# A two-step graph layer with guessed top-p thresholds: one store per pair of key and query tiles, sums stored a slot later, law constants by step with a round less, and the last products of a guess on VectorE

## The chip, the cores and the metric

The kernel runs on one core of one Trainium2 chip. The metric is the device time of one execution in microseconds (us). A core has five engines that each work through their own queue in order: PE (TensorE, matrix products; PEld is its weight load), DVE (VectorE), ACT (ScalarE), POOL (GpSimd) and SP (SyncE, which here only issues DMAs). They wait for each other through semaphores.

## The reference, cut to what matters

```
h = relu(layernorm(x))                       # x: 3327 x 256, adj: 3327 x 3327, sparse
R = (adj + I) / rowsum                       # fixed graph
for n in range(2):
    q = Xa @ W1.T @ W2.T ; k = Xa @ W3.T     # 64 columns each
    probs = softmax(q @ k.T)                 # 3327 x 3327
    A = the largest probs of each row until their sum reaches 0.9, renormalised
    Xf = R @ Xf ; Xa = A @ Xa
    Z += Xf @ U1[n].T + Xa @ U2[n].T
out = x + layernorm(h + Z)
```

For each row of the attention matrix the threshold has to be found from which on values are kept.

## The kernel before, in words

The 3327 rows are padded to 3328 and cut into 26 tiles of 128 rows (`NT` = 26). Two steps run one after the other, and each passes through the 26 tiles in slots of some 21 to 24 us, as a software pipeline in which several tiles are under way at once: exps of a later tile's logits (`weights`, L634 products on PE and L636 exp on ACT), the guess of the next tile (`measured_once` in step 0, `measured_twice` in step 1), the settling of the present one (`settle`), and the attention sum of the one before (`Sums`, L836 transposes and L849 products on PE). `settle` is where the exact threshold is found on DVE: one pass over the row block keeps in `w` what lies below the guess (L756), 20 MAX8 take the eight largest of each segment (L761), then rounds of MAX8 and MATCH_REPLACE (L768, L770) draw the largest 8 candidates at a time, 5 rounds in step 0 and 6 in step 1 (`ROUNDS`); a scan and three small operations (L775 to L780) find the boundary, and a second pass over the block masks it (L790). The guess itself is a law of the row's logarithm sum with constants `PG`, `PK`, `OFFSET`, `LNY`. In step 1 it has two stages: the last ones are ACT's third pass over the block (L660), two small operations on DVE (L726, L727), two on POOL (L724, L725: column 0 of `g`), three Ln-type operations on ACT (L729 to L731), two on DVE (L733, L734), five products on POOL (L735 to L739) and the exp on ACT (L741) that L756 waits for.

If a row's boundary isn't among the drawn candidates, a flag (`prove`) sends the whole program through `search_graph_layer`, a bisection of 27 rounds per tile.

In the opening a loop over `q` normalises x, and makes keys and queries of tile pairs: products on PE, `kq` copied on DVE, high parts cast on ACT, low parts subtracted on DVE. Each pair's raw queries go to `asks` (turned to the other half of the partitions) and its split queries to `qx` by DMAs on ACT's queue; `fetch` brings `qT` of a tile back. Meanwhile SP loads pieces of the adjacency (832 KB each at first), and DVE lists each row's nonzero blocks (`listed`, L879). After the opening the `products` (L1039 on PE) fill the free time of the first slots.

POOL also gathers (L926, L947: indirect DMAs that it issues itself), normalises the output (`finish`, L994 to L997 and L481 to L987), and adds `sv` (L972), which SP stores at once (L974).

In the slots the order on every engine is written by hand: `PLAN`, `BEGIN`, `OPEN` and `LAST` name for each of a slot's seven parts which generators (letters: m guess, d settle, f finish, g gather, s spread, e first_end, ...) go on by one `yield`, and every engine's instructions are tied to that order. In the opening a list scheduler places them.

Of the kernel before, what the change touches and what calls it, by code (L numbers as in the profile page):

```python
# [9 lines left out]
F32 = mybir.dt.float32  # L10
F32R = mybir.dt.float32r
# [3 lines left out]
AF = mybir.ActivationFunctionType  # L15
ALU = mybir.AluOpType
# [3 lines left out]
P = 128  # L20
N = 3327
# [293 lines left out]
LNBIG = 69.0  # L315
SEG = 168
NSEG = -(-NP // SEG)
ROUNDS = (5, 6)
PG = (0.72168716, 3.51308980, -3.48705157)
PK = (3.57528079, -2.54929187, 0.86603878)  # L320
OFFSET = (18.0, 14.0)
TOPK = 8 * max(ROUNDS)
LNY = 0.25 * math.log(0.72)

SQG, SQK = ((c[0], c[1] / (2 * c[0]), c[2] - c[1] ** 2 / (4 * c[0])) for c in (PG, PK))
HALF = NT // 2
# [10 lines left out]
AD = 4  # L337
# [10 lines left out]
def guess_graph_layer(ctx, tc, x, adj, w1t, w2t, w3t, u1t, u2t, ln_g, ln_b, out, flag):  # L348
    nc = tc.nc
# [74 lines left out]
    law = const.tile([P, 7, NT], F32, tag="law", name="law")  # L424
    one = const.tile([P, 8], F32, tag="one", name="one")
    for k, c in enumerate((1.0, -1.0, 5.0e-4, SQG[1], SQK[1], math.log(10.0), LNY, 1.0e-12)):
        G.memset(one[:, k : k + 1], c)
    of_s = const.tile([P, 4], F32, tag="of_s", name="of_s")
    for k, c in enumerate((SQG[0], SQG[2], -SQK[0], -SQK[2])):
        G.memset(of_s[:, k : k + 1], c)  # L430
    ones = const.tile([P, 1], F32, tag="ones", name="ones")
# [26 lines left out]
    kx = dram.tile([P, NP], F32, tag="kx", name="kx")  # L458
    qx = dram.tile([P, NP], F32, tag="qx", name="qx")
    qm = const.tile([P, 2, 2, 2 * DA + 2], F32, tag="qm", name="qm")  # L460
    G.memset(qm, 0.0)
# [96 lines left out]
    def project(step, t):  # L558
# [14 lines left out]
        G.tensor_tensor(col(2), col(1), half[:, 1:2], ALU.pow)  # L573
        G.tensor_scalar(ms[:, 3:7], of_s, col(2), 1.0e-4, ALU.mult, ALU.add)
        G.tensor_scalar(col(7), col(1), 0.5, minus, ALU.mult, ALU.subtract)
        G.tensor_scalar(col(7), col(7), 0.25, LNY - 0.25 * math.log(0.1 / N), ALU.mult, ALU.add)
        G.tensor_scalar(col(8), col(1), minus, col(4), ALU.subtract, ALU.add)
# [3 lines left out]
    def laws(ts):  # L581
# [19 lines left out]
        S.activation(s, s, AF.Exp, scale=0.5)  # L601
        for k, c in ((3, SQG[0]), (4, SQG[2]), (5, -SQK[0]), (6, -SQK[2])):
# [3 lines left out]
        G.tensor_scalar(m, m, 0.25, LNY - 0.25 * math.log(0.1 / N), ALU.mult, ALU.add)  # L606
        G.tensor_scalar(var, var, 0.125, None, ALU.mult)
# [34 lines left out]

    def guessed(r, g):
# [6 lines left out]
        S.activation(col(2), col(2), AF.Exp, scale=-1.0, bias=con(6))  # L650
        S.activation(col(3), col(2), AF.Square, bias=con(3))
# [10 lines left out]
    def measured_once(r):  # L662
        e, ms = r["e"], r["ms"]


        col = guessed(r, small.tile([P, 17], F32, tag="g", name="g"))
        S.activation(col(4), col(2), AF.Square, bias=con(4))
# [27 lines left out]
    def measured_twice(r):  # L695
# [3 lines left out]

        col = guessed(r, small.tile([P, 18], F32, tag="g", name="g"))  # L700
        S.activation(col(1), col(0), AF.Exp, scale=-1.0, bias=con(5))
# [32 lines left out]
        V.reciprocal(col(12), col(12))  # L734
# [4 lines left out]
        G.tensor_tensor(col(6), col(6), col(15), ALU.add)  # L739
        yield  # L740
# [222 lines left out]
    def first_end(t):  # L963
# [9 lines left out]
        yield  # L973
        nc.sync.dma_start(sx[t], sv)  # L974
        yield from prep(aT, t)
# [83 lines left out]
    scaled, turned, made, raw = {}, {}, {}, {}  # L1059
    for q in range(HALF + 5):  # L1060
        if 0 <= q - 3 < HALF:
            k, pk = q - 3, made.pop(q - 3)
            kq = row.tile([P, 2, P], F32, tag="s1", name="kq", bufs=4)
            qs = row.tile([P, 2, P], F32R, tag=("own", "xa")[k % 2], name="qs", bufs=2)
            V.tensor_copy(kq, pk[:, :2, :])
            raw[k] = kq, qs
            if 2 * k in COUNTED:
                V.tensor_copy(krs[:, k % 2, :DA], pk[:, 2, :DA])
# [33 lines left out]
        if 0 <= q - 3 < HALF:  # L1102
            kq, qs = raw[q - 3]
            S.copy(keys[low, 2 * (q - 3) * P : (2 * (q - 3) + 2) * P], kq[low].rearrange("p t r -> p (t r)"))
            S.copy(qs[high], kq[high])
        if 0 <= q - 4 < HALF:
            k, (kq, qs) = q - 4, raw[q - 4]
# [3 lines left out]
        if 0 <= q - 5 < HALF:  # L1111
            k, (kq, qs) = q - 5, raw.pop(q - 5)
# [16 lines left out]
        if q == 5:  # L1129
            for n in range(2):  # L1130
                nc.sync.dma_start(u1[:, :, n], u1t[n].rearrange("(c p) e -> p c e", p=P))
    moments(0, pgram[:DA, : DA + 1])
    for k in range(3):
# [201 lines left out]
```

## Time and profile before

| what | value |
| --- | --- |
| time, median of 3 runs | 1377.66 us (1375.54 to 1378.56) |
| the profiled execution, its own time | 1375.91 us |
| its span in the trace | 1374.2 us |
| busy: PE, DVE, ACT, POOL | 1237.3, 1197.8, 1074.3, 1026.1 us |
| mean granted TensorE clock | 0.972 |

The stages by the trace: opening until the first `w` (L756) at 93.1 us, the first slots with the products until 208 us, step 0 until about 762 us, step 1 from there, with its last `w` at 1326.6 us. In the page, part 1 gives the busy time of each engine, part 4 the chain of work that ended last, part 5 groups of instructions with mean durations in ns. A row of the chain or of the timeline begins with its start in us and its length in us.

### The profile page before, as it was taken

What the parts mean: (1) busy time and instruction counts of PE and PEld (TensorE: products, weight loads), DVE (VectorE), ACT (ScalarE), POOL (GpSimd) and SP (SyncE); (2) the same over time, 40 slices, a digit from 0 to 9 for tenths busy, and PEclk for the clock granted to TensorE, in tenths of its full rate; (3) what the DMA queues carried; (4) which work ended last, traced back from release to release, by engine and by line L of the source; (5) the groups of instructions that cost most, each with busy time, mean ns of one, the idle gap of its engine ahead of it and who ended that gap; (6) DMA issues with size and microseconds to landing.
All of it is one profiled execution on the core that took longest, in us unless ns stands there. A gap on an engine that the chain in (4) does not pass through costs nothing.

```text
span 1374.2 us, 22501 instructions
## 1 busy us (share of the span) xinstructions
PE 1237.3 (90%) x6340; PEld 1030.9 (75%) x6340; DVE 1197.8 (87%) x3662; ACT 1074.3 (78%) x2239; POOL 1026.1 (75%) x1437
## 2 busy tenths in 40 slices
PE   5769899999999999999999669898999999999985
PEld 4534688888887888888788558787878778787874
DVE  7757789999999999999892589898998999999993
ACT  4566688878787887878763689898998999998841
POOL 4123588888888888888785578888887888888842
PEclk9789999999999999999999869999999999999998
DMA  8644455555555555555544321322313133131200
GB/s 287 216 128 128 144 166 142 155 159 152 169 152 163 148 163 149 154 163 157 149 144 121 87 58 57 94 85 66 97 54 96 61 94 92 59 97 55 85 24 23
DMA packets 123192, 164.60 MB, mean 120 GB/s; under 512 B 21137, under 2 KB 89232, under 8 KB 123056
## 3 DMA queue, kind: packets, MB, share of 16 engines
q1 hardware_dynamic: 100608, 117.19, 27.4%
q0 software_dynamic: 16640, 42.69, 11.9%
q10 hardware_dynamic: 5808, 3.17, 0.8%
q8 instruction: 53, 0.87, 0.2%
q14 instruction: 83, 0.68, 0.2%
HBM read 128.74 MB, written 32.12 MB: 117 GB/s over the span
## 4 chain that ended last, share of the span: by engine, by line
DVE 53%; PE 17%; ACT 16%; POOL 7%; issue 4%; DMA 2%; SPq 0%; ACTq 0%; DVEq 0%; POOLq 0%
DVE cand L761 9%; ACT ja L660 9%; DVE w L756 8%; DVE e L790 8%; PE pa L849 6%; DVE fm L879 5%; DVE bb L768 4%; DVE cand L770 4%; PE pz L1039 2%; PE pl L634 2%; ACT e L636 2%; PE pt L836 2%; PE pr L955 2%; POOL g L739 1%; ACT eT L838 1%
## 5 line engine op out<-in xcount | busy, mean ns | idle before, releaser
L660 ACT ACTIVATE ja<-e,g 128x3328 uint8<-128x3328 f32 x106 | 325.9, 3075 | 0.1
L849 PE MATMUL pa<-x,eT 128*128 128x256 f32 x1352 | 321.9, 379 | 0.0
L849 PE MATMUL pa<-xw,eT 128*128 128x256 f32 x1352 | 318.3, 380 | 3.1 <-DVE s L979 3.1
L849 PEld LDWEIGHTS pa<-xw,eT 128*128 128x128 f32 x1352 | 251.5, 190 | 36.4 <-DVE s L979 5.0
L849 PEld LDWEIGHTS pa<-x,eT 128*128 128x128 f32 x1352 | 242.8, 190 | 25.5
L761 DVE MAX8 cand<-w 128x8 f32<-128x168 f32 (+1 forms) x1040 | 253.4, 317 | 0.0
L838 ACT COPY eT<-pt 128x512 f32<-128x512 f32 (+1 forms) x364 | 199.3, 555 | 58.7 <-PE pt L836 58.5
L947 POOL DMA_INDIRECT xg<-bx,index x130 | 192.8, 1483 | 51.5 <-issue 21.1
L836 PE MATMUL pt<-ident,e 128*128 128x128 f32 x1144 | 175.3, 276 | 46.3 <-DVE e L790 32.4
L634 PE MATMUL pl<-keys,qT 128*128 128x512 f32 (+1 forms) x832 | 198.9, 375 | 17.3 <-ACT e L636 12.2
L836 PEld LDWEIGHTS pt<-ident,e 128*128 128x128 f32 x1144 | 140.4, 144 | 87.1 <-issue 50.0
L926 POOL DMA_INDIRECT ac<-in_adj,index x130 | 159.8, 1229 | 57.5 <-ACT e L1045 16.3
L947 POOL DMA_INDIRECT xg<-vx,index x130 | 150.6, 1159 | 34.2 <-issue 33.2
L634 PEld LDWEIGHTS pl<-keys,qT 128*128 128x128 f32 x832 | 144.2, 194 | 42.0 <-ACT e L636 14.4
L636 ACT ACTIVATE e<-pl 128x832 f32<-128x832 f32 (+1 forms) x176 | 150.5, 862 | 31.4 <-PE pl L634 27.3
L756 DVE SCALAR_TENSOR_TENSOR w<-e,g 128x3328 f32<-128x3328 f32 x44 | 163.8, 3722 | 4.7 <-ACT g L741 4.6
L955 PE MATMUL pr<-xg,ac 128*128 128x257 f32 (+1 forms) x520 | 140.2, 394 | 10.0 <-DVE s L1162 8.4
L790 DVE SCALAR_TENSOR_TENSOR e<-e,rec 128x3328 f32<-128x3328 f32 x40 | 148.0, 3701 | 0.6
L955 PEld LDWEIGHTS pr<-xg,ac 128*128 128x128 f32 x520 | 96.3, 197 | 22.1 <-DVE s L1162 8.8
L768 DVE MAX8 bb<-cand 128x8 f32<-128x160 f32 x286 | 92.6, 324 | 6.4
L879 DVE TENSOR_REDUCE fm<-at 128x4 f32<-128x512 f32 (+1 forms) x133 | 84.3, 634 | 5.9 <-DMA at<-in_adj 5.9
L703 POOL TENSOR_SCALAR g<-g,law 128x1 f32<-128x1 f32 x23 | 65.8, 2862 | 10.9 <-ACT g L702 10.0
(261 smaller groups left out, 2018.6 us busy)
## 6 DMA issues: line engine op xcount, KB each, us to landing
at<-in_adj SPq DMA_DIRECT2D x114, 256.0 KB
cx<-ac SPq DMA_DIRECT2D x26, 384.0 KB
ac<-cx SPq DMA_DIRECT2D x26, 384.0 KB
wide<-in_adj SPq DMA_DIRECT2D x8, 832.0 KB
qT<-qx SPq DMA_DIRECT2D x196, 32.0 KB
e<-in_adj SPq DMA_DIRECT2D x6, 832.0 KB
own<-bx SPq DMA_DIRECT2D x26, 128.5 KB
x<-in_x SPq DMA_DIRECT2D x13, 256.0 KB
```

The lines of the kernel that those rows point to most:

```text
L634: PE.matmul(pl[:, a:b], qT[:, k, :], keys[:, c + a : c + b], start=k == 0, stop=k == 1)
L636: S.activation(e[:, c : c + w], pl[:, :w], AF.Exp, accum_out=za[:, n : n + 1])
L660: S.activation(ja, e, f, bias=guess, scale=sign, accum_out=total)
L756: V.scalar_tensor_tensor(w, e, col(16), e, ALU.is_lt, ALU.mult, accum_out=d2)
L761: V.max(cand[:, 8 * s : 8 * s + 8], w[:, s * SEG : min(NP, (s + 1) * SEG)])
L790: V.scalar_tensor_tensor(e, e, at(1), e, ALU.is_ge, ALU.mult, accum_out=ra)
L836: PE.transpose(pt[:, j, :], e[:, (j0 + j) * P : (j0 + j + 1) * P], ident)
L838: S.copy(eT[:, :w, :], pt[:, :w, :])
L849: PE.matmul(self.pa, eT[:, c - 4 * k, :], self.xa[:, c, :], start=c == 0, stop=c == NT - 1)
L926: G.indirect_dma_start(out=ac[:, k, :], out_offset=None, in_=rows, in_offset=bass.IndirectOffsetOnAxis(ap=index[:, t, k : k + 1], axis=0), ...
L947: G.indirect_dma_start(out=xg[:, k, :w], out_offset=None, in_=rows, in_offset=bass.IndirectOffsetOnAxis(ap=index[:, t, k : k + 1], axis=0))
L955: PE.matmul(pr[:, :w], ac[:, k, :], own if k == KT - 1 else xg[:, k, :w], start=k == 0, stop=k == KT - 1)
```

## The change

Five edits:

- A pair's raw and split queries now lie in one tile `both` of 2 KB a partition, and go to `rx` in one store per pair on SP, a pass of the loop later. `asks` is read back from `rx` (`recall`), `qT` of step 0 as well. `fetch` takes two DMAs instead of four. ACT issues no DMAs in the loop any more.
- The store of `sv` joins the list that SP works off in a later part of the slot (`stores`).
- `PG`, `PK`, `OFFSET`, `LNY` are given per step, and `ROUNDS` goes from (5, 6) to (4, 5).
- The five last products of the guess in step 1 move from POOL to DVE, with narrower bounds, and in another order.
- The first logits of tile 0 come one pass of the loop later.

```
-ROUNDS = (5, 6)
-OFFSET = (18.0, 14.0)
+ROUNDS = (4, 5)
+OFFSET = (16.0, 13.0)
...
-    def fetch(step, t, q2=None, by=nc.sync):
+    def fetch(step, t):
         qT = tpool.tile([P, 2, P], F32R, tag="qT", name="qT", bufs=3)
+        of = qx[:, t * P : (t + 1) * P] if step else rx[:, t // 2, 2 + t % 2, :]
         for rows in (low, high):
-            for k, half_ in enumerate((low, high)):
-                src = qx[half_, t * P : (t + 1) * P] if q2 is None else q2[half_].bitcast(F32)
-                by.dma_start(qT[rows, k, :].bitcast(F32), src)
+            nc.sync.dma_start(qT[rows].bitcast(F32), of.rearrange("(k p) r -> p k r", k=2))
+    def recall(a, b):
+        for h, rows in enumerate((high, low)):
+            nc.sync.dma_start(asks[rows, a:b, :], rx[high, a:b, h, :])
...
         V.reciprocal(col(12), col(12))
-        G.tensor_scalar(col(12), col(12), col(8), 0.7, ALU.mult, ALU.max)
-        G.tensor_scalar(col(11), col(12), 1.5, col(11), ALU.min, ALU.mult)
-        G.tensor_tensor(col(2), col(3), col(2), ALU.subtract)
-        G.tensor_scalar(col(15), d1, col(0), LNBIG, ALU.is_lt, ALU.mult)
-        G.tensor_tensor(col(6), col(6), col(15), ALU.add)
+        V.tensor_scalar(col(12), col(12), col(8), 0.85, ALU.mult, ALU.max)
+        V.tensor_scalar(col(11), col(12), 1.2, col(11), ALU.min, ALU.mult)
+        V.tensor_scalar(col(15), d1, col(0), LNBIG, ALU.is_lt, ALU.mult)
+        V.tensor_tensor(col(6), col(6), col(15), ALU.add)
+        V.tensor_tensor(col(2), col(3), col(2), ALU.subtract)
...
-        nc.sync.dma_start(sx[t], sv)
+        stores.append((sx[t], sv))
...
-    for q in range(HALF + 5):
+    for q in range(HALF + 6):
...
-            kq = row.tile([P, 2, P], F32, tag="s1", name="kq", bufs=4)
-            qs = row.tile([P, 2, P], F32R, tag=("own", "xa")[k % 2], name="qs", bufs=2)
+            both = (tpool.tile([P, 4, P], F32, tag="eT", name="both", bufs=3) if k % 5 < 3 else
+                    adjp.tile([P, AD, P], F32, tag="at", name="both", bufs=2))
...
-            for h in range(2):
-                nc.scalar.dma_start(query_of(2 * k + h), kq[high, h, :])
-            nc.scalar.dma_start(qx[:, 2 * k * P : (2 * k + 2) * P], qs.bitcast(F32).rearrange("p t r -> p (t r)"))
-            for h in range(2):
-                if 2 * k + h < 3:
-                    fetch(0, 2 * k + h, qs[:, h, :], nc.scalar)
+        if 0 <= q - 6 < HALF:
+            nc.sync.dma_start(rx[:, q - 6], raw.pop(q - 6)[0])
+        if q in (7, 8):
+            for t in range(2 * (q - 7), 4 * q - 26):
+                fetch(0, t)
+        if q == 15:
+            recall(0, 7)
...
-        if q == 6:
+        if q == 7:
             run(begun[0], 1)
```

Lines move by 5 or 6 in the changed file, so before's L724, L725, L734, L790 are its L729, L730, L739, L795. On SP, in the opening, this stood before (x is the input, wide and e hold pieces of the adjacency, u is a weight):

```order
L389 DMA x_95<-in_x 128x2x256 x13
L869 DMA wide<-in_adj 128x1664 x2
L1131 DMA u_138<-in_u1t 128x2x256 x2
L869 DMA e_101<-in_adj 128x1664 x2
L869 DMA wide<-in_adj 128x1664 x2
L869 DMA e_101<-in_adj 128x1664 x2
```

and this stands there now, with a store of a pair behind each piece of the adjacency:

```order
L874 DMA e_101<-in_adj 128x1664
L1118 DMA rx<-both 128x512
L874 DMA e_101<-in_adj 128x1664
L1118 DMA rx<-both 128x512
L551 DMA qT<-rx 64x2x128 x4
L874 DMA wide<-in_adj 128x1664
L1118 DMA rx<-both 128x512
L551 DMA qT<-rx 64x2x128 x2
```

So loads, stores and fetches now share one queue in the opening. On DVE, in a slot of step 1, this stood behind the reciprocal of the guess before (bb and cand are the candidates of `settle`; in brackets, whom the instruction waits for):

```order
L734 RECIPROCAL g<-g 128x1 [waits DVE_49]
L768 MAX bb<-cand 128x8
L770 MATCH_REPLACE cand<-bb,cand 128x160 [waits DVE_49]
L768 MAX bb<-cand 128x8 [waits DVE_49]
L770 MATCH_REPLACE cand<-bb,cand 128x160 [waits DVE_49]
L768 MAX bb<-cand 128x8 [waits DVE_49]
```

and this stands there now:

```order
L739 RECIPROCAL g<-g 128x1 [waits DVE_49]
L740 TENSOR_SCALAR g<-g 128x1 [waits DVE_49,Pool_49]
L741 TENSOR_SCALAR g<-g 128x1 [waits DVE_49,Pool_49]
L742 TENSOR_SCALAR g<-g 128x1 [waits Pool_49]
L743 TENSOR_TENSOR g<-g 128x1 [waits DVE_49]
L744 TENSOR_TENSOR g<-g 128x1 [waits Activation_49]
L773 MAX bb<-cand 128x8
L775 MATCH_REPLACE cand<-bb,cand 128x160 [waits DVE_49]
L773 MAX bb<-cand 128x8 [waits DVE_49]
```

One round has gone from behind them, and the products stand in DVE's queue ahead of the rest of `settle`. What they wait for on POOL is, in its own queue now, the end of this piece (rstd and nm belong to the output's normalisation, xg to the gathers):

```order
L952 DMA xg<-vx,index 128x256 [waits DMASW6_49]
L721 TENSOR_SCALAR g<-g 128x1 [waits Activation_49]
L722 TENSOR_SCALAR g<-g 128x1
L723 TENSOR_SCALAR g<-rec,g 128x1 [waits DVE_49]
L724 TENSOR_SCALAR g<-g 128x1
L483 TENSOR_SCALAR rstd<-mv 128x1 [waits DVE_49]
L484 TENSOR_TENSOR rstd<-rstd,half 128x1 [waits Pool_49]
L992 TENSOR_SCALAR nm<-mv,rstd 128x1 [waits Pool_49]
L729 TENSOR_SCALAR g<-oa 128x1 [waits Activation_49]
L730 TENSOR_SCALAR g<-rec,g 128x1 [waits Pool_49]
```

The piece is as it was; only the five products that followed it have gone from POOL.

More of the change, by code (lines that the diff above doesn't have):

```diff
@@ L424, in guess_graph_layer @@
     law = const.tile([P, 7, NT], F32, tag="law", name="law")
-    one = const.tile([P, 8], F32, tag="one", name="one")
-    for k, c in enumerate((1.0, -1.0, 5.0e-4, SQG[1], SQK[1], math.log(10.0), LNY, 1.0e-12)):
+    one = const.tile([P, 10], F32, tag="one", name="one")
+    for k, c in enumerate((1.0, -1.0, 5.0e-4, SQG[0][1], SQK[0][1], math.log(10.0), LNY[0], 1.0e-12, SQG[1][1], LNY[1])):
         G.memset(one[:, k : k + 1], c)
-    of_s = const.tile([P, 4], F32, tag="of_s", name="of_s")
-    for k, c in enumerate((SQG[0], SQG[2], -SQK[0], -SQK[2])):
-        G.memset(of_s[:, k : k + 1], c)
+    of_s = const.tile([P, 2, 4], F32, tag="of_s", name="of_s")
+    for step in range(2):
+        for k, c in enumerate((SQG[step][0], SQG[step][2], -SQK[step][0], -SQK[step][2])):
+            G.memset(of_s[:, step, k : k + 1], c)
     ones = const.tile([P, 1], F32, tag="ones", name="ones")
@@ L638, in weights, with guessed @@
                 yield
-    def guessed(r, g):
+    def guessed(r, g, step):
         r["col"] = col = lambda k: g[:, k : k + 1]
@@ L663, in measured_once @@
         e, ms = r["e"], r["ms"]
-        col = guessed(r, small.tile([P, 17], F32, tag="g", name="g"))
+        col = guessed(r, small.tile([P, 17], F32, tag="g", name="g"), 0)
         S.activation(col(4), col(2), AF.Square, bias=con(4))
@@ L696, in measured_twice @@
         e, ms = r["e"], r["ms"]
-        col = guessed(r, small.tile([P, 18], F32, tag="g", name="g"))
+        col = guessed(r, small.tile([P, 18], F32, tag="g", name="g"), 1)
         S.activation(col(1), col(0), AF.Exp, scale=-1.0, bias=con(5))
@@ L1131, in guess_graph_layer @@
                 nc.sync.dma_start(u1[:, :, n], u1t[n].rearrange("(c p) e -> p c e", p=P))
+    recall(7, HALF)
     moments(0, pgram[:DA, : DA + 1])
```

30 lines of the change are left out of this document (15 added, 15 removed).

## The prediction

> **What bounds the kernel now.** I read the page's chain of work first, to see which engine ended last, and then the busy time by stage, cut at the `w` passes (L756) that open the slots.
>
> ```profile
> span 1374.2 us, 22501 instructions
> DVE 53%; PE 17%; ACT 16%; POOL 7%; issue 4%; DMA 2%; SPq 0%; ACTq 0%; DVEq 0%; POOLq 0%
> ```
>
> ```profile
> 0.00:93.10 93.10, 58.17 (x238) 41.08 (x238) 66.18 (x196) 48.57 (x102) 28.87 (x120) 0.88 0.72 229
> 93.10:208.30 115.20, 107.95 (x458) 76.37 (x459) 88.31 (x262) 82.28 (x189) 62.14 (x78) 0.96 0.45 135
> 208.30:663.40 455.10, 443.69 (x2382) 376.69 (x2380) 439.21 (x1372) 376.92 (x891) 385.22 (x461) 1.00 0.55 156
> 663.40:808.00 144.60, 115.46 (x585) 95.95 (x585) 97.92 (x343) 93.19 (x201) 98.68 (x142) 0.90 0.39 113
> 808.00:1326.60 518.60, 479.25 (x2519) 413.07 (x2518) 480.30 (x1416) 465.70 (x845) 441.56 (x621) 0.99 0.25 76
> ```
>
> A row has the stretch, its length, the busy time of PE, PEld, DVE, ACT and POOL, the granted clock, the DMA share and GB/s. No engine bounds the opening alone. From 93 to 208 us PE is full (107.95 of 115.20). In step 0 the chain runs on DVE, but PE is idle only 455.10 - 443.69 = 11.41 us in 19 slots: two engines are near their bound. Step 1 runs from 808.0 to 1326.6 us in 24 slots, 518.60 / 24 = 21.61 us each (24 by the count of a group shown below), with DVE busy for 480.30 of it.
>
> The sum below is made against the profiled execution, 1375.9 us (its span and 1.7 us around it). The median of the runs is 1.8 us higher, and I add that at the end.
>
> **Step 0: a round less.** A round stands in the chain of step 0 like this:
>
> ```profile
> 208.39 3.62 DVE w L756 x2
> ...
> 224.60 0.40 DVE cand L770 x2
> 225.00 0.02 issue
> 225.02 0.34 DVE bb L768
> 225.36 0.02 issue
> ...
> 232.35 3.62 DVE w L756 x2
> ```
>
> The change takes 0.40 + 0.02 + 0.34 + 0.02 = 0.78 us from each slot of 23.96 (232.35 - 208.39). If DVE alone decided, 19 slots would give 14.8 us. PE's transposes show what is late next:
>
> ```profile
> L836 PE MATMUL pt<-ident,e 128*128 128x128 f32 x494 | 76.8, 275 | 11.4 <-DVE e L790 7.2 <-ACT kq L515 4.3
> ```
>
> Nearly all of PE's idle time in these slots, 11.4 us, lies before this group, and 7.2 us of it ends with DVE's mask. A faster DVE can shrink that part; the 4.3 us that end with ACT stay, unless ACT's work comes earlier with DVE's. So the gain is between 4 us, should PE's waits shrink by half, and 11.4 us; I take 6, a little under the 7.2.
>
> **Step 0: the sums stored later.** One slot at the end of step 0 is longer:
>
> ```profile
> 639.40:663.40 24.00, 24.00 (x132) 20.41 (x130) 23.14 (x74) 19.64 (x45) 18.09 (x22) 1.00 0.52 147
> 663.40:690.50 27.10, 22.55 (x120) 18.82 (x120) 22.87 (x66) 20.02 (x49) 23.38 (x28) 1.00 0.51 146
> ```
>
> ```profile
> 664.08 4.19 POOL sv L972
> 668.29 0.32 SPq L974
> ...
> 671.15 3.63 DMA at<-in_adj
> 674.80 0.69 DVE fm L879
> ```
>
> SP stands behind the sum `sv`, which POOL finishes late, and the piece of the adjacency behind it reaches DVE late. With the store moved to the later part of the slot, SP issues that load without waiting for `sv`; queued behind the store afterwards are the key and query stores of the same list, which nothing in the slot waits for. What can go is the slot's excess of 27.10 - 24.00 = 3.1 us; PE was idle 27.10 - 22.55 = 4.55 there, so PE lets it go. I take 3, with 0 as the other end. In the other slots the load isn't late and the move costs and gives nothing: SP waits hide behind buffers already loaded. So step 0 gives 9.
>
> **The opening.** The chain of the opening waits for DMAs five times:
>
> ```profile
> 22.57 4.49 DMA asks<-kq
> 28.39 6.84 DMA qT<-qs
> 35.26 2.04 DMA qT<-qs
> 46.54 4.08 DMA asks<-kq
> 55.01 2.40 DMA asks<-kq
> ```
>
> ```profile
> 0.00:34.00 34.00, 20.11 (x85) 14.49 (x86) 24.04 (x77) 13.76 (x28) 15.92 (x78) 1.00 0.87 286
> 34.00:69.00 35.00, 25.45 (x112) 19.77 (x113) 28.12 (x80) 20.39 (x43) 6.43 (x20) 0.76 0.69 216
> ```
>
> They are 19.85 us, the most that could go. Of these the 8.88 of `qT` are the plainest: the fetches were issued on ACT, so ACT stood still with its copies, and now SP does it. The other three are waits for a buffer whose store hasn't landed; the new tile has such a wait too. The queues themselves set the other bound. By the two rows 34 x 286 + 35 x 216 KB, 17.3 MB, moved in the first 69 us. The change adds 64 KB to each of 13 pairs and reads 0.85 MB back for `asks`, but one piece of the adjacency (0.85 MB) comes after the loop now instead of in it: 18.1 MB, which at 286 GB/s take 63 us. So of the 69 us about 6 can go. SP then holds the rest of `recall` behind a fetch that waits for tile 0's products, so the later side is 0, or a loss of 4 (one late DMA such as the 4.08). I take a gain of 6, and keep -4 to 15.
>
> The rule that speaks against this edit is in the Trainium skill, "DMA: Bandwidth & Descriptors", section "Queues, rings and completion order": a DMA engine takes turns between queues packet by packet, but works through one queue's ring in order. By that rule a store on ACT's queue took turns with the loads, and on SP's it lies behind the pieces of the adjacency issued ahead of it, so the opening would gain nothing; that is the second rival below, which I price from rows.
>
> **Step 1: the products on DVE.** This is the term that turns the sign. The chain of one slot, and POOL and ACT beside it:
>
> ```profile
> 958.85 3.60 DVE w L756 x2
> 972.73 0.16 DVE g L734
> 975.84 3.70 DVE e L790 x2
> 979.73 3.60 DVE w L756 x2
> ```
>
> ```profile
> 958.92 3.60 POOL L704 TENSOR_SCALAR g<-g 128x1 f32<-128x1 f32 x1
> ...
> 973.99 0.27 POOL L725 TENSOR_SCALAR g<-rec,g 128x1 f32<-128x1 f32 x1
> ...
> 995.23 0.27 POOL L725 TENSOR_SCALAR g<-rec,g 128x1 f32<-128x1 f32 x1
> ...
> 996.86 3.55 POOL L739 TENSOR_TENSOR g<-g 128x1 f32<-128x1 f32 x1
> ```
>
> ```profile
> L725 POOL TENSOR_SCALAR g<-rec,g 128x1 f32<-128x1 f32 x24 | 6.5, 270 | 2.4
> L727 DVE TENSOR_SCALAR g<-g 128x1 f32<-128x1 f32 x24 | 5.1, 214 | 0.8
> 976.77 0.28 ACT L702 ACTIVATE g<-g,one 128x1 f32<-128x1 f32 x1
> ```
>
> What the move removes: in the next slot L739, an operation on one column, runs while DVE does L790, and takes 3.55 us; `w` then starts late. Without such a delay a slot is 979.73 - 958.85 = 20.88 us, so at most 0.73 of the mean 21.61 hangs on it.
>
> What it adds: a wait. Of the five products now on DVE, the third (before's L738, the flag of `d1`) reads the column that POOL's L725 writes. In the shown slot the reciprocal L734 ends at 972.89, and L725 ends at 974.26. DVE fills 0.43 us with the first two products (two small operations of 0.214), then stands until 974.26, some 0.9 us; queued behind are the last two rounds, the scan, the mask L790, and the next `w`. Until now POOL bore this wait, and DVE did three rounds meanwhile.
>
> The new slot, counted from its `w` at 958.85: L725 ends at 974.26; three more products 0.64 bring 974.90. From the reciprocal to L790 there were 975.84 - 972.89 = 2.95 us; a round less makes 2.17, so the mask starts at 977.07. From mask to `w` it is 3.89 as before: 980.96. The slot is 22.11 us, 0.50 over the mean, and 24 slots lose 12.0 us. ACT isn't late: the exp L741 comes behind L702, which ended at 977.05, and `w` needs it at 980.96. The slot's shape also holds for the next slot: L703 on POOL starts after L702, at 977.05, so it is caught by the mask again, L704 by `w`, and POOL's row of operations up to L725 starts after `w`'s end as it did in the shown one.
>
> The bounds: if POOL came early enough that DVE never waits, the slot is 20.88 - 0.78 + 5 x 0.214 = 21.17, a gain of 10.6. If every slot is like the next one (`w` at 979.73, L725 ending at 995.50), it is 995.50 + 0.64 + 2.17 + 3.89 - 979.73 = 22.47, a loss of 20.6. I take the middle one, since the row of POOL's operations between `w` and L725 is not touched by the change.
>
> At the two ends of the steps one more slot each, outside the counted ones, loses its 0.78 us of a round; with the narrower scan behind it I take 2 us. The law's constants change no instruction count. Worked through with the reference's inputs in double precision, at most 30 values are drawn until the boundary in step 0 (of 32) and 35 in step 1 (of 40), so the second program isn't entered. If it were, each of its rounds has a pass like this one:
>
> ```profile
> L660 ACT ACTIVATE ja<-e,g 128x3328 uint8<-128x3328 f32 x106 | 325.9, 3075 | 0.1
> ```
>
> and 27 rounds x 26 tiles x 2 steps x 3.075 us alone are 4317 us.
>
> **The sum.** -6 (opening) - 9 (step 0) - 2 (ends) + 12 (step 1) = -5 us: 1370.9 for the profiled execution, some 1372.5 as a median; I give 1372.
>
> **The rivals.**
>
> 1. *DVE is held longer in step 1* (slower). The mechanism is the same wait, at the price of the later slots: 22.47 us each, 20.6 in place of 12, so 1381; with an opening that gives nothing, 1387. It decides from 22.3 us a slot (a loss of 17 eats the other terms). For it: L725 comes 1.37 us behind the reciprocal in one slot and 1.73 in the next. Against: the later one follows from a late L703, which itself follows from products on POOL that go.
> 2. *The opening gains nothing* because the stores lie behind the loads in one queue: a piece of 832 KB takes 2.9 us at 286 GB/s, and a pair's tile, one of five, is written again when its store has landed. The price is the opening's 6 us, so 1378, no change. For it: the DMA share of 0.87 in the first 34 us. Against: the share of 0.69 behind that.
> 3. *DVE doesn't wait in step 1*, since POOL has five operations less per slot and gets ahead: -10.6 in place of +12, 1350. For it: POOL is idle 518.60 - 441.56 = 77 us in 24 slots, so it isn't full. Against: its operations from `w`'s end to L725 follow each other and DVE's two long passes stop it.
> 4. *The second program is entered*, since the law misses a row: 1372 + 4317, over 5,600 us. Against it are the counts above; nothing in the profile is for it.
>
> **How the numbers follow.** My forecast has 0.42, the first rival 0.25, the second 0.20, the third 0.12, the fourth 0.01. A measurement of this kernel can tell about 0.2%, 2.8 us, from no change. Of the forecast's own range (1364 to 1380) 0.30 lie below 1374.9, 0.08 within, 0.04 above; of the second rival 0.06, 0.08 and 0.06; of the first 0.02 within and 0.23 above; the third is faster. That gives faster 0.48, same 0.18, slower 0.34. The range takes in the first rival to 1386 and the opening's better end (9 us more), with part of the third: 1357 to 1386.
>
> **What the profile after would show.** Step 0: slots of 23.5 to 23.7 us, and PE's idle time before L836 down from 11.4 us by half or more. The slot at 663 us as long as its neighbours. Opening: the first `w` at some 87 us, with no wait of ACT for `qT`. Step 1: idle time of DVE before the product that reads POOL's column, 0.8 to 1.0 us in each of 24 slots, released by that POOL operation, slots of 22.1 us, and no POOL operation of 3.55 us in the guess's products. Wrong it would be made by that idle time being near 0 (then rival 3), or by slots of 22.4 us and more (rival 1).

## The result, and the profile after

The changed kernel takes 1385.18 us (median of 5 runs, 1383.64 to 1387.28), the kernel before 1376.80 us beside it (1375.54 to 1378.56). The ratio is 1.006, with a 95% interval of 1.0045 to 1.0075: the change makes the kernel slower by 8.4 us. The forecast was 1372 us. The profiled execution of the changed kernel took 1385.18 us, so nothing has to be added to its trace.

The first lines of the page of the changed kernel, with the chain's shares by engine:

```profile
span 1383.5 us, 22295 instructions
DVE 43%; PE 26%; ACT 11%; POOL 4%; issue 3%; DMA 1%; SPq 0%; DVEq 0%; ACTq 0%; POOLq 0%
```

DVE's share fell from 53% to 43%, PE's rose from 17% to 26%: the path moved, but did not become shorter. The stages of the changed kernel, cut at the same `w` passes as before (the columns are those of the prediction):

```profile
0.00:98.70 98.70, 65.24 (x256) 43.69 (x257) 66.66 (x196) 55.00 (x120) 30.24 (x130) 0.84 0.70 233
98.70:204.30 105.60, 98.35 (x432) 70.49 (x431) 86.83 (x252) 74.68 (x165) 59.70 (x73) 0.98 0.52 152
204.30:655.80 451.50, 442.99 (x2367) 375.79 (x2366) 429.66 (x1315) 375.79 (x892) 382.56 (x458) 0.99 0.56 157
655.80:804.10 148.30, 122.21 (x610) 101.57 (x609) 96.47 (x341) 94.49 (x207) 102.65 (x141) 0.89 0.38 108
804.10:1336.70 532.60, 490.86 (x2516) 426.44 (x2515) 479.76 (x1465) 470.11 (x844) 413.73 (x495) 0.96 0.25 74
```

Read against before's rows: the fifth `w` comes at 204.3 instead of 208.3; the 19 slots of step 0 take 451.5 instead of 455.1; what lies between them and step 1's slots 148.3 instead of 144.6; the 24 slots of step 1 532.6 instead of 518.6. By the terms of the prediction, in us (step 0 counted over its 21 slots up to the last `w`, 503.55 before and 500.89 after; the ends are the passage between the steps and what follows the last `w`):

| term | forecast | measured |
| --- | --- | --- |
| opening, up to the fifth `w` | -6 | -4.0 |
| step 0 (a round 6, the late slot 3) | -9 | -2.7 |
| ends of the steps | -2 | +2.0 |
| step 1, 24 slots | +12 | +13.9 |
| sum | -5 | +9.3 |

**Step 1** has the wait that was worked out, in about half of its slots. Three rows of DVE's timeline in a slot whose `w` starts at 1116.54, and the group of the waiting product:

```profile
1131.07 0.21 DVE L741 TENSOR_SCALAR g<-g 128x1 f32<-128x1 f32 x1
1132.04 0.21 DVE L742 TENSOR_SCALAR g<-g 128x1 f32<-128x1 f32 x1 [0.76 <-POOL g L730]
...
1134.63 3.69 DVE L795 SCALAR_TENSOR_TENSOR e<-e,rec 128x3328 f32<-128x3328 f32 x1
```

```profile
L742 DVE TENSOR_SCALAR g<-g 128x1 f32<-128x1 f32 x24 | 5.0, 209 | 11.7 <-POOL g L730 11.7
```

DVE stands 0.76 us in that slot in front of the third product until POOL's column arrives, and everything behind it, the mask L795 and the next `w`, is late by that. It does so in 13 of the 24 slots, 11.7 us in all; most of these 13 last 21.9 us. In ten slots, one of the 13 among them, DVE waits for PE before it takes over PE's sums `pa` (a line of waits has the us in total, the times and the longest):

```profile
DVE s L984 <- PE pa L854: 12.5, 10, 2.0
```

Each of these ten begins with a low granted clock, behind a pause of 2.0 us or more in which PE waits for the late mask. This is PE in the slot that follows the one above, and the first 4 us of that slot:

```profile
1138.47 1.48 PE L841 MATMUL pt<-ident,e 128*128 128x128 f32 x8 [2.02 <-DVE e L795]
```

```profile
1138.50:1140.50 2.00, 2.00 (x10) 1.90 (x11) 2.00 (x2) 1.10 (x2) 1.93 (x2) 0.62 0.00 0
1140.50:1142.50 2.00, 2.00 (x8) 1.71 (x8) 1.94 (x4) 1.03 (x3) 1.92 (x2) 0.53 0.00 0
```

It lasts 22.3 us. The mean of all 24 is 22.19 us; 22.11 were forecast, from the first wait alone.

**The opening**: SP's longest wait for another engine, and DVE's two waits for the adjacency, until the first `w`:

```profile
SPq L551 <- PE pl L639: 13.0, 1, 13.0
```

```profile
DVE fm L884 <- DMA e<-in_adj: 8.2, 1, 8.2
...
DVE fm L884 <- DMA wide<-in_adj: 4.7, 1, 4.7
```

The change also fetches the queries of tiles 3 to 5 in the opening, which their slots fetch anyway. The fetch for tile 3 needs tile 0's buffer, so SP stands 13.0 us until PE has done tile 0's products, and the pieces of the adjacency behind it come late. The 8.2 us are new; a wait for a piece in `wide` stood in the kernel before too (4.2 us). The first `w` starts at 98.7, not at 87.

**Step 0** has three long slots, at 463, 629 and 656 us (25.5, 27.1 and 26.4 us), where before had one. POOL's addition of the identity in the slot ahead of the second of them and in it, then DVE's mask and ACT's waiting operation in it, by the timeline:

```profile
621.36 0.49 POOL L937 TENSOR_TENSOR ac<-ac,ident 128x128 f32<-128x128 f32 x1
...
645.89 3.69 POOL L937 TENSOR_TENSOR ac<-ac,ident 128x128 f32<-128x128 f32 x1
```

```profile
645.58 3.68 DVE L795 SCALAR_TENSOR_TENSOR e<-e,rec 128x3328 f32<-128x3328 f32 x1
```

```profile
650.10 0.29 ACT L685 ACTIVATE g<-oa,g 128x1 f32<-128x1 f32 x1 [5.63 <-POOL g L676]
```

POOL's addition began 0.31 us after DVE's mask and ended 0.32 us behind it, after 3.69 us instead of 0.49. Behind it on POOL are four small operations of the guess (L675 to L678); ACT waits 5.63 us for one of them, and its copies for PE stand behind that. In before the last of these four ended 4.4 us or more ahead of the mask in every slot of step 0; in the changed kernel the distance shrinks during step 0 to 0.7 us (0.3 in one slot), and in the three long slots at least one of the four is behind the mask (ends of L678 and starts of L795 in the trace). I call an operation that begins during such a pass and ends with it "caught" below.

### The profile page after: what moved, and what is told of

The parts are those of the page before. It is cut to its first block, busy times and chain, and to the rows that moved or that the text cites. A ratio compares the mean times of both kernels' runs of the same rounds, so it can differ in the third digit from the quotient of the medians.

```text
span 1383.5 us, 22295 instructions
## 1 busy us (share of the span) xinstructions
PE 1252.5 (91%) x6340; PEld 1046.1 (76%) x6340; DVE 1184.5 (86%) x3636; ACT 1077.7 (78%) x2239; POOL 998.5 (72%) x1313
## 3 DMA queue, kind: packets, MB, share of 16 engines
q0 software_dynamic: 16640, 42.69, 12.5%
## 4 chain that ended last, share of the span: by engine, by line
DVE 43%; PE 26%; ACT 11%; POOL 4%; issue 3%; DMA 1%; SPq 0%; DVEq 0%; ACTq 0%; POOLq 0%
PE pa L854 11%; DVE cand L766 8%; DVE e L795 7%; DVE w L761 7%; ACT ja L665 6%; PE pl L639 4%; PE pt L841 4%; PE pr L960 3%; DVE fm L884 3%; DVE bb L773 2%; DVE x L795 2%; DVE cand L775 2%; PE pz L973 1%; ACT e L641 1%; ACT eT L843 1%
## 5 line engine op out<-in xcount | busy, mean ns | idle before, releaser
L854 PE MATMUL pa<-x,eT 128*128 128x256 f32 x1352 | 326.0, 383 | 0.0
L854 PEld LDWEIGHTS pa<-x,eT 128*128 128x128 f32 x1352 | 245.0, 192 | 26.4
L931 POOL DMA_INDIRECT ac<-in_adj,index x130 | 219.0, 1685 | 57.8 <-ACT e L1050 16.6
L639 PE MATMUL pl<-keys,qT 128*128 128x512 f32 (+1 forms) x832 | 210.2, 390 | 19.5 <-ACT e L641 15.1
L841 PE MATMUL pt<-ident,e 128*128 128x128 f32 x1144 | 178.8, 280 | 40.3 <-DVE e L795 28.2
L841 PEld LDWEIGHTS pt<-ident,e 128*128 128x128 f32 x1144 | 144.4, 147 | 78.7 <-issue 56.2
L639 PEld LDWEIGHTS pl<-keys,qT 128*128 128x128 f32 x832 | 152.5, 204 | 45.0 <-ACT e L641 15.8
L952 POOL DMA_INDIRECT xg<-bx,index x130 | 147.1, 1131 | 51.2 <-issue 19.3
L761 DVE SCALAR_TENSOR_TENSOR w<-e,g 128x3328 f32<-128x3328 f32 x44 | 162.8, 3699 | 0.6 <-ACT g L746 0.5
L952 POOL DMA_INDIRECT xg<-vx,index x130 | 128.7, 990 | 37.5 <-issue 34.1
L795 DVE SCALAR_TENSOR_TENSOR e<-e,rec 128x3328 f32<-128x3328 f32 x40 | 147.2, 3680 | 0.6
L709 POOL TENSOR_SCALAR g<-g 128x1 f32<-128x1 f32 x26 | 79.9, 3075 | 1.8
```

The costliest lines, as they stand in the source:

```text
L639: PE.matmul(pl[:, a:b], qT[:, k, :], keys[:, c + a : c + b], start=k == 0, stop=k == 1)
L761: V.scalar_tensor_tensor(w, e, col(16), e, ALU.is_lt, ALU.mult, accum_out=d2)
L795: V.scalar_tensor_tensor(e, e, at(1), e, ALU.is_ge, ALU.mult, accum_out=ra)
L841: PE.transpose(pt[:, j, :], e[:, (j0 + j) * P : (j0 + j + 1) * P], ident)
L854: PE.matmul(self.pa, eT[:, c - 4 * k, :], self.xa[:, c, :], start=c == 0, stop=c == NT - 1)
L931: G.indirect_dma_start(out=ac[:, k, :], out_offset=None, in_=rows, in_offset=bass.IndirectOffsetOnAxis(ap=index[:, t, k : k + 1], axis=0), ...
```

## The experiments

Times are medians, beside runs of the kernel before on the same chip (1374.6 to 1376.7 us). The changed kernel itself wasn't run again beside them, so a difference to its 1385.18 us is uncertain by some 2 us, the spread of these.

**1. The fetch in the opening.**

```
-            for t in range(2 * (q - 7), 4 * q - 26):
+            for t in range(2 * (q - 7), q - 5):
```

> The changed kernel, but after the eighth pass of the opening loop only tile 2's queries are fetched, no longer those of tiles 2 to 5; tiles 3 to 5 are fetched in their slots, as they are anyway. In the changed kernel SP stood 13.0 us with the fetch for tile 3 (its buffer is tile 0's until tile 0's products are done), with two pieces of the adjacency behind it, and DVE then waited 8.2 and 4.7 us for these pieces, while the guess of tile 0 was ready at some 85 us. Theory A (this fetch is what cost the opening): DVE's two waits are gone, the first w starts at 86 to 89 us in place of 98.7, and, since PE has most of its work of the first slots still before it, the whole gains 4 to 10 us: 1375 to 1381. Theory B (the opening is held by the stores lying behind the loads in one queue): the pieces come late as before, first w at 96 us or later, 1383 to 1386.

1378.46 us (1369.87 to 1380.44, 10 runs; ratio to before 1.0003, 0.9985 to 1.0022): 6.7 us less than the changed kernel. SP's wait is gone, the first `w` is at 91.1 and the fifth at 198.2, 10 us earlier than in the kernel before. Theory A, though 91.1 isn't the 86 to 89 expected: DVE still waits 4.4 us for one piece, about as in the kernel before. The three long slots of step 0 stayed.

**2. The products back on POOL.**

```
-        V.tensor_scalar(col(12), col(12), col(8), 0.85, ALU.mult, ALU.max)
+        G.tensor_scalar(col(12), col(12), col(8), 0.85, ALU.mult, ALU.max)
...
-        V.tensor_tensor(col(2), col(3), col(2), ALU.subtract)
+        G.tensor_tensor(col(2), col(3), col(2), ALU.subtract)
```

> The changed kernel with the five products of the guess in step 1 back on POOL, in the changed order and with the changed bounds; all else as in the changed kernel. Theory A (DVE's wait for POOL's column costs): DVE goes on with its rounds behind the reciprocal at 14.0 us of the slot, so that the mask starts at 16.1 instead of 18.0; POOL's products then begin at 15.4 and the second or third of them is caught by the mask until 19.8, and w starts at 20.9 to 21.1: slots of 21.0 in place of 22.19, 24 slots give 28 us, 1357. Theory B (a POOL product caught by the mask costs as much as the wait): slots of 21.6 to 22.2, 1371 to 1385. Theory C (nothing is caught): slots of 20.1 to 20.5 with PE as the bound, 1335 to 1345.

1364.51 us (ratio 0.9922, 0.9902 to 0.9942): 20.7 us less than the changed kernel. The slots last 21.43 us. POOL and DVE in one of them, and ACT's exp that closes the guess:

```profile
944.70 3.65 POOL L742 TENSOR_SCALAR g<-g 128x1 f32<-128x1 f32 x1
```

```profile
944.49 3.69 DVE L795 SCALAR_TENSOR_TENSOR e<-e,rec 128x3328 f32<-128x3328 f32 x1
```

```profile
L746 ACT ACTIVATE g<-g 128x1 f32<-128x1 f32 x26 | 10.0, 386 | 25.4 <-POOL g L744 25.4
```

In about every second slot the mask catches a product, and ACT stands for it in order, 25.4 us in all. So the move to DVE has a reason, but its price (22.19) is above what it saves (21.43). The result lies between theories A and B: A's mechanism, at a smaller gain than its 28 us.

**3. The products behind the last rounds.**

```
-        V.reciprocal(col(12), col(12))
+        V.reciprocal(col(12), col(12)); yield
...
-            ("llcmss", "lnms", "lwwnfd", "lcmdsssgggg", "fdsmwqdf", "llmdf", "lmwdg"))
+            ("llcmss", "lnms", "lwwnfd", "lcmdsssgggg", "fdsmwqdf", "llmdf", "lmwdmg"))
```

(The same letter m is added in the first two slots.)

> The changed kernel with the five products still on DVE, but behind the last two rounds, the scan and the three small operations after it, in place of ahead of them, so that DVE does these while POOL makes the column that the third product reads. Theory A (the loss is the wait): no idle time of DVE ahead of that product (0.76 us before), the mask starts at 17.1 us of the slot instead of 18.0, slots of 20.9 to 21.2, 24 slots give 24 us at most: 1361 to 1366. Theory B (the loss is DVE's added work, five small operations a slot): the slots stay at 22.0 to 22.2, 1382 to 1386.

1352.56 us (1345.08 to 1353.23; ratio 0.9833, 0.9816 to 0.9849): 32.6 us less than the changed kernel, more than either theory said.

```profile
L742 DVE TENSOR_SCALAR g<-g 128x1 f32<-128x1 f32 x26 | 5.3, 205 | 0.2 <-issue 0.2
```

```profile
798.40:1297.40 499.00, 475.17 (x2516) 412.66 (x2515) 472.12 (x1465) 464.66 (x845) 395.49 (x496) 0.99 0.27 79
```

The same instructions in another order: the wait for POOL is gone, the 24 slots take 499.0 instead of 532.6 us, 20.79 each. PE's busy time fell by 15.7 us with them, and its granted clock is 0.99 instead of 0.96. DVE's 12.5 us of waits for PE are gone as well; the two groups of waits were 24.2 of the 33.6 us. It was the wait for POOL and what followed from it, not DVE's added work.

**4. The rounds and the law alone**, on the kernel before:

```
-ROUNDS = (5, 6)
-OFFSET = (18.0, 14.0)
+ROUNDS = (4, 5)
+OFFSET = (16.0, 13.0)
...
-        G.tensor_scalar(col(12), col(12), col(8), 0.7, ALU.mult, ALU.max)
+        G.tensor_scalar(col(12), col(12), col(8), 0.85, ALU.mult, ALU.max)
```

> The kernel before with the law's constants by step, a round less in each step and the narrower bounds of the two products (these still on POOL, in their old order); the opening, the stores of the sums and the engines as before. Theory A (in step 0 PE takes over, and a mask that comes earlier catches POOL's operations): step 0 gains 2 to 5 us, with two or three slots of 26 to 27 us; step 1 as in the changed kernel with the products on POOL, slots near 21.0, a gain of 12 to 15: 1357 to 1363. Theory B (a round less is worth its 0.78 us in every slot): 35 us in 45 slots, 1342. Theory C (nothing is gained in step 1, since the mask catches POOL's products in every slot): 1372 to 1375.

1367.22 us (ratio 0.9937, 0.992 to 0.9953), 9.5 us less. Step 0 takes 499.2 us, with slots of 26.5, 26.5 and 27.7; step 1's slots 21.52, against 21.61. A round less gave step 1 next to nothing, since POOL's products are caught: one of them lasts over 3 us in 12 of 24 slots, against 8 in the kernel before. In two of step 0's long slots POOL's sum `sv` was caught by `w` and SP, which stores it at once, stood behind it: the stall that the prediction had seen in one slot.

```profile
491.80 4.18 POOL L973 TENSOR_TENSOR sv<-sv,x 128x256 f32<-128x256 f32 x1
```

**5. The products alone**, on the kernel before (the five lines of run 2 the other way round, old bounds):

> The kernel before with nothing changed but the five last products of the guess, which go to DVE in the change's order (with the old bounds, and six rounds in step 1 as before). Theory A (DVE's wait for POOL's column is what costs): DVE stands 0.8 us in front of the third product and has three rounds behind it: the mask starts at 18.8 us of the slot, w at 22.7, slots of 22.7 to 23.1, 24 slots lose 26 to 36 us: 1403 to 1413. Theory B (only the work of five small operations moves to DVE, 1.07 us a slot): slots of 21.95, a loss of 8 us: 1385.

1406.15 us (ratio 1.0219, 1.02 to 1.0237), 31.6 us more; the slots last 22.90 us. Theory A.

**6. The identity added a gather earlier**, in the changed kernel:

```
-            if k == KT - 2:
+            if k == KT - 3:
                 G.tensor_tensor(ac[:, KT - 1, :], ac[:, KT - 1, :], ident, ALU.add)
```

> The changed kernel, but POOL adds the identity to the gathered diagonal block one gather earlier, so that this addition no longer stands right ahead of the four operations of the guess that ACT waits for in step 0. Theory A (the late slots of step 0 are those in which DVE's mask catches a POOL operation of that row): the slots at 629 and 656 us go from 27.1 and 26.4 to 23.2 to 24.0, the one at 463 us from 25.5 to 24 or less; step 0 gains 6 to 9 us: 1376 to 1379. Theory B (something else holds these slots, a DMA or SP): they stay as long, 1383 to 1387.

1387.16 us (ratio 1.0081, 1.0062 to 1.0099): no gain. The long slots moved to 394, 420, 539 and 661 us, and the mask catches the next operations of the same row:

```profile
411.89 3.69 POOL L677 TENSOR_SCALAR g<-g 128x1 f32<-128x1 f32 x1
```

Neither theory: what is caught follows from where POOL's row lies against the mask, and taking one operation out of its path only changes which one it is.

**7. The sums stored later, alone**, on the kernel before:

```
-        nc.sync.dma_start(sx[t], sv)
+        stores.append((sx[t], sv))
```

> The kernel before with nothing changed but the store of the sums, which joins the list that SP works off later in the slot. Theory A (the prediction's term: the slot at 663 us is late since SP stands behind the sum): that slot goes from 27.0 to 24, 1373 to 1374. Theory B (POOL's late sum is itself only a result of the gathers on POOL and of DVE's passes, and the load behind it isn't what decides): the slot stays at 26 us or more, 1376 to 1378.

1369.28 us (ratio 0.995, 0.993 to 0.9969), 5.3 us less. The slot at 663 us lasts 23.3 instead of 27.0. Theory A: alone, this edit does what the prediction said. The slot is 3.7 of the 5.3 us; where the rest comes from was not tested.

**8. Three edits together**: those of runs 1, 3 and 6.

> The changed kernel with three edits at once: tile 2's fetch alone in the opening, the products behind the last rounds on DVE, the identity added one gather earlier. If the three causes are independent, their gains add up: 1352.6 as the median with the products last, less 7 for the fetch, less 6 to 9 for the addition: 1337 to 1340. If the opening's gain is lost again behind PE, which is full in the slots that follow: 1343 to 1347.

1346.26 us (ratio 0.9786, 0.9757 to 0.9815): the opening's gain adds to that of the products, the addition gives nothing (four long slots again).

**9. The four operations of step 0's guess on ACT**, in the changed kernel:

```
-        G.tensor_scalar(col(7), col(9), 0.5, None, ALU.mult)
+        S.activation(col(7), col(9), AF.Copy, scale=0.5)
...
-        G.tensor_scalar(col(10), col(9), col(5), 1.0, ALU.mult, ALU.add)
+        S.activation(col(10), col(9), AF.Identity, scale=col(5), bias=con(0))
```

> The changed kernel, but the four operations of the guess of step 0 that POOL did in front of ACT's chain are done by ACT itself; nothing of the guess then stands on POOL behind the gathers. Theory A (the late slots of step 0 come from a POOL operation of that row that DVE's mask catches, and ACT and PE wait for it): no slot of step 0 over 25 us, and PE loses neither its idle time there nor the slow products after it: step 0 gains 6 to 12 us, 1373 to 1379. Theory B (ACT's copies for PE come later by the four operations, 1.1 us a slot, and PE waits for these instead): 1385 to 1391.

1368.40 us (ratio 0.9946, 0.9929 to 0.9962): 16.8 us less than the changed kernel, beyond theory A. The 19 slots of step 0, and PE's transposes in them:

```profile
202.80:646.70 443.90, 443.46 (x2376) 376.15 (x2376) 426.64 (x1317) 386.53 (x968) 360.58 (x389) 1.00 0.57 161
```

```profile
L841 PE MATMUL pt<-ident,e 128*128 128x128 f32 x493 | 76.4, 274 | 0.0
```

No slot is over 25 us. PE is idle 0.4 us in 443.9: now PE is the bound, and with the same work on PE step 0 can't become shorter by other engines' work.

**10. The best version**: the edits of runs 1, 3 and 9.

> The changed kernel with tile 2's fetch alone in the opening, the products on DVE behind the last rounds, and the four operations of step 0's guess on ACT. With the first two and the addition moved, the median was 1346.3 with four late slots in step 0. Theory A (late slots gone): 1335 to 1341. Theory B (ACT's four operations cost PE as much): 1344 to 1350.

1327.39 us (1326.78 to 1328.12; ratio 0.9654, 0.9638 to 0.967), 57.8 us less than the changed kernel and 48 us less than the kernel before: theory A, and some 8 us under its range. Its chain:

```profile
PE 46%; DVE 31%; ACT 15%; issue 3%; DMA 2%; POOL 2%; SPq 0%; DVEq 0%; ACTq 0%; POOLq 0%
```

**11. The opening alone**: the changed kernel with the old law and rounds, the products on POOL and the sums stored at once, so

```
-ROUNDS = (4, 5)
+ROUNDS = (5, 6)
...
-        stores.append((sx[t], sv))
+        nc.sync.dma_start(sx[t], sv)
```

> The kernel before with the opening of the changed kernel alone (one store per pair on SP, the fetches and the reading back on SP), with the old law, the old rounds, the products on POOL and the sums stored at once. Theory A (the opening's edit is a gain of its own, though the fetch for tile 3 holds SP): the first w is late, at 97 to 99 us, the fifth w 3 to 5 us earlier than before's 208.3, the whole 1370 to 1373. Theory B (what the opening gains, PE or the last slots of step 0 take back): 1374 to 1377.

1373.57 us (ratio 0.9987, 0.9977 to 0.9996), 2.0 us less. First `w` at 98.2, fifth at 205.6: a small gain, in spite of SP's stop, and a time between the two theories.

**12. The four operations on ACT and on POOL**: as in run 9, and POOL does them as well, for nobody:

```
+        G.tensor_scalar(spare[:, 0:1], col(9), 0.5, None, ALU.mult)
...
+        G.tensor_scalar(spare[:, 3:4], col(9), spare[:, 2:3], 1.0, ALU.mult, ALU.add)
```

> The kernel with the four operations of step 0's guess on ACT (1368.4 us), but POOL does the same four operations as well, at their old place, into columns that nobody reads. Theory A (what cost was ACT's and PE's wait for an operation of this row that DVE's mask catches): POOL's copies of them may be caught, but nobody waits for them: no slot of step 0 over 25 us, 1366 to 1371. Theory B (what cost was POOL's load: with slots of 23.3 us POOL, gaps between its gathers included, falls behind, and the gathers or the sums are late): late slots come back, 1375 to 1386.

1386.83 us (ratio 1.0094, 1.0076 to 1.0112): the whole gain of run 9 is lost, though nobody waits for these four. In the changed kernel POOL's lateness reached PE by ACT's wait; this run shows that the loss doesn't need that wait. By the waits of its trace it goes here by way of SP and the gathers. In the 19 slots SP stands 42.0 us in front of stores that wait for POOL's `lo` and `gsum` (run 9 has no such wait there), and DVE waits for pieces of the adjacency that SP issues:

```profile
DVE fm L884 <- DMA at<-in_adj: 7.5, 6, 1.9
```

Right behind them PE stands for a late gather:

```profile
PE pr L960 <- DMA xg<-bx,index: 6.0, 2, 5.8
```

Theory B: POOL's load. POOL has little room in the changed kernel's step 0: of its 68.9 us without work in the 19 slots (451.50 - 382.56), 54.9 stand in front of its gathers:

```profile
L931 POOL DMA_INDIRECT ac<-in_adj,index x92 | 164.6, 1789 | 25.1 <-issue 10.0 <-ACT eT L843 3.4 <-ACT g L690 1.8
L952 POOL DMA_INDIRECT xg<-bx,index x95 | 106.8, 1124 | 29.8 <-issue 14.4 <-ACT g L686 4.7 <-ACT eT L843 4.6
```

That is 0.29 us a gather, in 187 gathers (the timeline shows a gap of 0.26 to 0.31 us ahead of most). Some 14 us are left in 19 slots: busy time, with the caught stretches in it, and gaps nearly fill the slot.

**13 and 14. POOL's relief without and with the round less**, on the kernel before: the four operations on ACT; then the same with the edits of run 4.

> The kernel before with nothing changed but the four operations of step 0's guess, done by ACT instead of POOL. Theory A (DVE's chain with five rounds bounds step 0, POOL lies right behind it): the slots stay at 23.9 to 24.0 us and only the late slot at 663 us may go: 1371 to 1375. Theory B (POOL bounds step 0 already): slots of 23.3 us, 10 to 14 us less: 1361 to 1365.

> The kernel before with the round less and the law's constants by step (products on POOL, as in the earlier run, 1367.2 us) and the four operations of step 0's guess on ACT. Theory A (two bounds, one behind the other, and both have to go): slots of 23.3 us in step 0 and none over 25: 9 to 12 us less than 1367.2: 1355 to 1358. Theory B (the late slots of that run come from the sums stored at once, which this run keeps): late slots stay, 1361 to 1367.

1369.91 us (ratio 0.996, 0.9949 to 0.9972) and 1352.39 us (0.983, 0.9803 to 0.9858). Theory A's mechanism in both, at times a little under its ranges. The time of step 0's 21 slots, in us, from four profiles, one each:

| step 0 | five rounds | four rounds |
| --- | --- | --- |
| four operations on POOL | 503.6 (before) | 499.2 (run 4) |
| four operations on ACT | 501.1 (run 13) | 488.7 (run 14) |

Either edit alone gives 2.5 to 4.4 us, both 14.8: DVE's chain and POOL's row bound step 0 one behind the other.

## Why the prediction failed, and where it was right

**Step 0 is the step that failed.** It gave 2.7 of its 9 us, the largest part of the 14.3 us by which the sum was off. The prediction took 6 us for a round less, "between 4 us, should PE's waits shrink by half, and 11.4 us", since PE is next to DVE, and 3 us for the late slot. PE's waits ahead of its transposes did shrink, from 11.4 us to 0.8 in the 19 slots, but in the changed kernel PE waits elsewhere there, for copies of ACT's that stand behind ACT's waits for POOL:

```profile
PE pq L567 <- ACT eT L843: 7.6, 5, 4.2
```

PE as the floor was right: with POOL relieved, the 19 slots take 443.9 us, 11.2 less than before, close to the 11.4 it gave as the most. But it missed an engine that stands ahead of PE. Step 0's sum has no term for POOL, though the row has it busy for 385.22 us of 455.10; of the 69.9 us that seem free, 55.9 are gaps in front of gathers. With slots of 23.3 us instead of 23.9 POOL can't keep pace, its row slides towards the mask, operations are caught, and three long slots give back most of what the round gave. The late slot's 3 us were right by themselves (run 7); they were lost to the same cause.

**Step 1 was right in its mechanism, and its size is in part luck.** The third product waits for POOL, but in 13 of 24 slots and mostly by 0.76 us, where some 0.9 us in each were forecast. With 21.91 us in all of them, as in the slot shown, step 1 would have lost some 7 us by my estimate, (21.91 - 21.61) x 24. PE's low clock behind its pauses, and DVE's waits for PE that come of it, weren't in the prediction; with them it is 22.19 us a slot against 22.11 forecast, 13.9 us against 12. That they come of DVE's lateness rests on run 3, where both groups of waits go together. The first rival would have needed 22.47. The median lies in that rival's range (1381 to 1387), but not by its mechanism; that the forecast's own range (1357 to 1386) holds it is owed to the room left for that rival.

**The opening** came out at 4.0 of its 6 us. It was priced with a later side of 4 us for "a fetch that waits for tile 0's products"; that fetch cost 6.7 us of the whole time. Without it the fifth `w` comes 6.1 us earlier still (204.3 to 198.2, run 1), so the rest of the edit would have gained 10. The late side was too small, and a wait of SP's was priced by what SP holds, not by the pieces behind it. The second rival, with the rule of the Trainium skill ("DMA: Bandwidth & Descriptors", section "Queues, rings and completion order") behind it, didn't decide: SP waited 0.5 us in all for a stored pair, and DVE's waits until the first `w` name no store. What came late was held by SP's own wait ahead of the issue, not by the order within a ring.

**The ends** cost 2.0 us instead of gaining 2. The passage from step 0 to step 1 took 77.1 us instead of 74.5. It was 74.6 to 76.8 in runs 13, 9, 10 and 14, without long slots, and 81.9 in run 12, where POOL was furthest behind, so POOL's lateness has a part in it; how much was not tested apart.

**The fourth rival** didn't come about in the changed kernel, nor in any run of an experiment. One execution of the kernel before, beside run 12, took 7184.82 us, where the six others took 1374.09 to 1380.51; it isn't part of that run's ratio. That is 5,810 us more, over the 4317 us that the prediction put on the second program's passes. No profile of it was kept, so whether it entered the second program isn't known.

**The edits add up** only roughly: alone they give -2.0, -5.3, -9.5 and +31.6 us, together +14.8, where the change gave +8.4. The round less and the products act on the same waits.

## What to carry to other kernels

Before an operation is moved to the engine on the critical path, look at who writes its inputs and what is queued behind it; here the same five operations cost 32.6 us more ahead of the last rounds than behind them. An engine that is 85% busy can be full: add the gaps in front of its DMA issues, and remember that its busy time holds the stretches in which another engine stops it, which can grow. When the critical engine gets faster, check which engine's row then meets its long passes, since the gain is paid back there.

## What the runs showed of the hardware

POOL's operations that begin during a DVE pass with two tensor inputs last until that pass ends. In the changed kernel 57 of POOL's compute operations began with more than 1 us of such a pass (L761, L795) left; none of them was shorter than 1.5 us, and alone they take 0.2 to 0.8 us (59 in the kernel before, none shorter either). They ended 0.05 to 0.59 us behind the pass. The Trainium skill, "SBUF — State Buffer", section "Who interferes with whom", says that a DVE instruction with two inputs from SBUF contends with a GpSimd instruction that reads SBUF, over a shared port pair that is an exclusive lock; these rows agree. Gathers are held too: of 40 that began so in the changed kernel, 39 took over 3.2 us (median of all 3.82), where one alone takes 0.96.

A pause of PE can cost more than its length. In the long slot at 629 us PE stood 4.17 us; the granted clock (the third column from the right) of two 2-us stretches after it, and of a later one:

```profile
654.00:656.00 2.00, 2.00 (x8) 1.65 (x7) 1.02 (x10) 1.93 (x6) 1.68 (x2) 0.57 0.48 149
656.00:658.00 2.00, 2.00 (x8) 1.65 (x8) 2.00 (x1) 0.00 (x0) 1.71 (x1) 0.58 0.17 45
658.00:660.00 2.00, 2.00 (x16) 1.87 (x15) 1.96 (x4) 1.04 (x4) 2.00 (x1) 1.00 0.00 0
```

Eight products of the same line took 3.34 us right after the pause and 1.73 us later, by the chain of waits:

```profile
654.33 3.34 PE pa L854 x8
...
659.03 1.73 PE pa L854 x8
```

The Trainium skill, "TensorE: Matmul & The Clock Gate", section "Part 1: The HAM clock gate", says that the clock falls to half after an idle window of about 3.4 us; the 4.17 us and the 0.57 agree. Other pauses here don't: in step 1 of the changed kernel the clock fell behind pauses of 2.0 us (0.62 and 0.53 in the slot shown with the result), and in step 0 of run 4 it stayed at 1.00 behind pauses of 2.0, 2.6 and 3.3 us. So the length of a pause alone doesn't decide it here.
